# Own places in the timetable for the first and last samples, shares on ScalarE, and four statistics ahead of the branch

## The chip, the cores and the metric

The kernel runs on one core of a Trainium2 chip. The metric is the device time of one execution in microseconds. An execution contains one launch; the profiled execution gives both its own time and the span from its first to its last recorded instruction.

## The reference

The input `x` has 16 samples of 256 channels and 64x64 pixels, in float32. Two layers are computed, each added to its input. Both begin with a group normalisation (32 groups of 8 channels).

```python
def _L0_conv_ref(x, g_norm, w_qkv, w_out, b_out, g_out):   # linear attention
    xn = rmsnorm(x, g_norm)                                # over channels
    qkv = einsum('oc,bchw->bohw', w_qkv, xn)               # 3 x 4 heads x 32
    q = softmax(q, axis=-2); k = softmax(k, axis=-1)
    context = einsum('bhdn,bhen->bhde', k, v)
    out = einsum('bhde,bhdn->bhen', context, q * scale)
    return rmsnorm(einsum('oc,bchw->bohw', w_out, out) + b_out, g_out)

def _L1_conv_ref(x, router_w, router_b, dw_w, dw_b, pw_w, pw_b):
    prob = softmax((mean(x, axis=(2, 3)) @ router_w.T + router_b) / 2.0)
    # the best 2 of 4 experts per sample; each expert:
    #   depthwise 3x3 convolution + bias, gelu, 256x256 pointwise + bias
    # the output is their sum, weighted by the renormalised probabilities

x = x + _L0_conv_ref(_gn(x), ...)
x = x + _L1_conv_ref(_gn(x), ...)
```

## The kernel before, in words

A short head loads sample 0 into the ring, scales the query, key and value weights, and tests whether the attention logits are small enough. A branch then runs `pipelined_path`, which is the path taken here.

Everything in that path is one list of steps. A step belongs to a sample `b` and to one of five phases. Phases `in`, `q` and `out` go over eight tiles `g` of 512 pixels; phase `route` is once a sample; phase `x` goes over four quarters `j` of 1024 pixels.

- `in`: `load_a`, `stats` (one `bn_stats` per 128 channels, L264), then `mean` to `bias`, the scale and bias of the first group norm.
- `q`: `load_b`; `norm` (L305 on VectorE or L307 on ScalarE); transposes `turn_x` (L315); `x_sq` (L322) and `token` (VectorE, then a power on GpSimd, L242), which make the scale `r` of a pixel; `x_keep` (L331 or L333), `project` (L346), `evacuate` (the exponential, L354), `context` (L364), `q_sum` (L374), `q_norm` on GpSimd (L379), `q_turn` (L387) and `q_keep` (L390). After the last tile `mix_a` to `mix_c` make one matrix `mw` of the context and the output weights.
- `out`: `load_x1` into the ring, `attend` (L440), `out_sq` (L448), `out_scale` (L241 and GpSimd L242), `out_norm` (L461 on ScalarE or L463 on VectorE), `out_turn` (L468), `out_add` (L477), `sq_sums` (L484).
- `route`: second group norm, router, and the choice of taps.
- `x`: channels 0 to 127 get their depthwise convolution on TensorE: `pad0` (ScalarE), `lay` and `spread` (DMAs through DRAM), `conv` (L719), `gelu0` (L727). Channels 128 to 255 get it on VectorE: `pad1`, `start`, and eight `tap` steps for each of two experts (L741, 1024 pixels each), then `gelu1` (L750). `pick` mixes the pointwise weights of the four experts; `lay_pw` and `spread_pw` lay half of them out; `pw` is the pointwise matmul (parts 0 and 1 at L768, parts 2 and 3 with 32 rows at L779), `residual` adds bias and input, `store` writes.

There is one order for all engines: every step has a place, and the steps are issued in the order of their places. Each engine, and SP's queue of DMAs, then works through its own instructions in that order. A place is counted in units of which a tile has `SLOT` = 8 and a sample 64:

```python
    def place(row):
        phase, b, g, key = row[:4]
        pace = 1 if phase in ("route", "x") else slots[b][phase] / SLOT
        return starts[b][phase] + slots[b][phase] * g + PLAN[key] * pace
```

`PLAN` holds one number for each kind of step, the same for all samples, and offsets for whole phases of the first three samples and the last two. So while sample `b` is in its phase `x`, the `out` phase of `b+1` or `b+2` and the `q` phase of `b+2` or `b+3` are in progress. The first samples have nothing ahead of them to overlap with, and the last have nothing behind.

Three shares depend on the sample. `norm` and `x_keep` are on VectorE for samples below `EARLY` = 3, else on ScalarE. `out_norm` is on VectorE except in the last sample. In the last sample the input is added by TensorE in a fifth part of `pw` (part 4, a matmul with the identity, L774), and `residual` is an activation on ScalarE (L793) in place of the add on VectorE (L795).

Of the kernel before, what the change touches and what calls it, by code (L numbers as in the profile page):

```python
# [10 lines left out]
FP = mybir.dt.float32  # L11
# [5 lines left out]
P = 128  # L17
# [30 lines left out]
EARLY = 3  # L48
# [5 lines left out]
    "load_x1": 2.47, "mean": 1.04, "means": 4.69, "dev": 5.07, "devs": 8.24, "scale": 8.52,  # L54
    "bias": 12.08, "in_lead": 22.23, "norm0": -5.91, "norm1": -3.77, "turn_x0": 0.61, "x_sq0": 1.9,
    "x_sq1": 2.11, "turn_x1": 1.64, "x_sq2": 2.36, "x_sq3": 2.68, "token": 3.59, "x_keep0": 5.41,
    "x_keep1": 5.42, "x_keep2": 5.2, "x_keep3": 5.22, "project0": 3.62, "evacuate0": 5.48,
    "project1": 4.85, "evacuate1": 5.69, "project2": 5.61, "evacuate2": 6.6, "project3": 5.69,
    "evacuate3": 6.83, "context": 7.87, "q_sum": 8.01, "q_norm": 13.4, "q_turn": 15.77,
    "q_keep": 16.04, "mix_a": 8.41, "mix_turn": 9.67, "mix_v": 10.33, "mix_vv": 11.49, "mix_b": 12,  # L60
    "mix_out": 12.87, "mix_c": 13.33, "mix_lead": 15.68, "attend0": -0.16, "out_sq0": 0.33,
    "out_sq1": 0.7, "out_scale0": 1.35, "out_norm0": 2.44, "attend1": 0.39, "out_sq2": 1.3,
    "out_sq3": 1.47, "out_scale1": 2.38, "out_norm1": 3.76, "out_turn0": 4.83, "out_add0": 6.02,
    "sq_sums0": 6.68, "out_turn1": 5.56, "out_add1": 6.85, "sq_sums1": 7.24, "sums1": 7.53,
    "means1": 7.77, "scale1": 8.7, "router": 9.48, "route": 9.99, "choose": 12.08,
    "pick_taps": 16.41, "route_lead": 22.29, "pick_rows0": 12.27, "pick_rows1": 15.38,
    "pick_row_bias": 13.7, "weigh": 19.29, "pick_bias": 20.19, "pick000": 1.5, "pick100": 11.76,
    "pick001": 2.67, "pick101": 11.83, "pick002": 5.78, "pick102": 15.2, "pick003": 8.9,
    "pick103": 15.49, "pick010": 1.98, "pick110": 13.36, "pick011": 3.58, "pick111": 15.09,
    "pick012": 4.61, "pick112": 15.41, "pick013": 6.8, "pick113": 16.18, "lay_pw": 10.27,  # L70
    "spread_pw": 12.95, "taps0": 6.17, "taps1": 1.71, "taps2": 2.27, "taps3": -4.16, "taps4": 9.52,
    "taps5": -1.21, "taps6": -1.21, "taps7": 11.56, "pad1": -10.11, "start0": -3.22, "tap01": 0.77,
    "tap02": 1.13, "tap03": 1.92, "tap04": 2.35, "tap05": 2.68, "tap06": 3.77, "tap07": 5.22,
    "tap08": 6.68, "gelu10": 10.88, "start1": 3.82, "tap11": 5.21, "tap12": 6.65, "tap13": 8.35,
    "tap14": 9.77, "tap15": 11.78, "tap16": 12.05, "tap17": 13.11, "tap18": 13.97, "gelu11": 15.52,
    "pad00": 1.66, "pad01": 2.92, "lay": 4.37, "spread0": 6.43, "conv0": 10.64, "gelu00": 11.57,
    "spread1": 6.19, "conv1": 11.39, "gelu01": 12.09, "spread2": 5.8, "conv2": 10.58,
    "gelu02": 11.06, "spread3": 6.79, "conv3": 12.01, "gelu03": 12.46, "spread4": 6.78,
    "conv4": 13.04, "gelu04": 14.02, "spread5": 7.96, "conv5": 13.16, "gelu05": 14.2,
    "spread6": 9.37, "conv6": 13.42, "gelu06": 14.64, "spread7": 10.33, "conv7": 13.97,  # L80
    "gelu07": 14.66, "pw00": 16.91, "pw01": 17.04, "pw02": 18.17, "pw03": 18.59, "pw10": 19.2,
    "pw11": 20.88, "pw12": 21.41, "pw13": 21.48, "residual00": 20.87, "residual01": 25.47,
    "residual02": 27.17, "residual03": 27.67, "store0": 29.36, "residual10": 23.57,
    "residual11": 25.64, "residual12": 27.45, "residual13": 28.04, "store1": 33.91,
    "in_first": 2.74, "in_more": 1.74, "q_first": 9.11, "out_first": 7.86, "out_more": 15.48,
    "q_less": 0.26, "load_a0": -16.2, "load_a1": -8.65, "load_b0": -17.65, "load_b1": -7.1,
    "stats0": -4.87, "stats1": -3.45, "load_weights": 21.49, "scale_weights": -2.89,
    "spread_taps00": -8.7, "spread_taps01": -1.56, "spread_taps10": 1.5, "spread_taps11": 5.1,
    "end_pw00": 16.45, "end_pw01": 18.13, "end_pw02": 14.45, "end_pw03": 15.46,
    "end_residual00": 23.47, "end_residual01": 25.21, "end_residual02": 26.09,  # L90
    "end_residual03": 28.08, "end_pw10": 17.51, "end_pw11": 19.09, "end_pw12": 14.97,
    "end_pw13": 16.08, "end_residual10": 28.63, "end_residual11": 28.83, "end_residual12": 29.05,
    "end_residual13": 30.35, "x_0": -0.07, "x_1": -0.03, "x_2": -0.04, "x_e1": -0.24, "x_e2": -0.02,
    "route_0": 1.22, "route_1": -0.07, "route_2": 0, "route_e1": 0.66, "route_e2": 0.04,
    "out_0": -0.91, "out_1": 0.05, "out_2": -0.02, "out_e1": 0.4, "out_e2": 0.22, "q_0": -0.72,
    "q_1": 1.29, "q_2": 0.04, "q_e1": -0.03, "q_e2": 0, "in_0": 8.12, "in_1": 4.22, "in_2": 0.93,
# [1454 lines left out]
```

## Time and profile before

| | |
|---|---|
| time, median of 3 runs | 2724.26 us (2723.83 to 2724.53) |
| the profiled execution's own time | 2722.39 us |
| its span | 2720.7 us |
| mean granted TensorE clock | 0.992 |
| TensorE busy | 2636.2 us, 97% |
| VectorE busy | 2417.5 us, 89% |
| ScalarE busy | 2083.4 us, 77% |
| GpSimd busy | 767.4 us, 28% |
| DMA moved | 394.77 MB, mean 145 GB/s |

Below, PE is TensorE, DVE is VectorE, ACT is ScalarE, POOL is GpSimd and SP is the queue that issues the DMAs. A line of the groups gives the source line, engine, operation, output and input tiles with their shapes, the number of instructions, the busy time with the mean of one in ns, and the idle time just before them with what ended most of it. A line of the waits reads "who waited <- for whom: us in total, times, longest". A line of the timeline starts with start and duration. Matmuls are pipelined, so their durations overlap; the spacing of starts is the real cost. A float32 matmul leaves two records, a transpose one.

### The profile page before, as it was taken

How to read it: one execution, taken by the hardware profiler on the slowest of the kernel's cores; microseconds unless marked ns; L12 is line 12 of the kernel's file. 1: busy time of each engine (PE TensorE's matmuls, PEld its weight loads, DVE VectorE, ACT ScalarE, POOL GpSimd, SP SyncE). 2: the span in 40 equal slices, each digit the busy share in tenths (PEclk: the TensorE clock that was granted, in tenths of full speed). 3: DMA queues.
4: the chain of work that ended last, by engine and by line, in shares of the span. 5: the costliest groups of instructions: out<-in, count | busy, mean ns of one | idle time of the engine just before them, and what ended most of it. 6: DMA issues, size and time to landing. Idle time of an engine off the chain costs nothing.

```text
span 2720.7 us, 55294 instructions
## 1 busy us (share of the span) xinstructions
PE 2636.2 (97%) x19300; PEld 2257.1 (83%) x19300; DVE 2417.5 (89%) x4480; ACT 2083.4 (77%) x5230; POOL 767.4 (28%) x874
## 2 busy tenths in 40 slices
PE   6898999999999999999999999999999999998888
PEld 5787888888888888888888888888888888886677
DVE  6889998999989898898989989898898988889984
ACT  3576788887887888788787888888788788876543
POOL 2242232322323222232322323233222323232200
PEclk9999999999999999999999999999999999999989
DMA  4335454454545546355354545445454443525332
GB/s 155 113 125 148 141 170 153 133 167 155 154 146 158 158 144 184 129 162 170 125 170 153 155 155 158 155 143 173 143 159 154 145 135 123 150 85 140 118 110 89
DMA packets 229711, 394.77 MB, mean 145 GB/s; under 512 B 25904, under 2 KB 108336, under 8 KB 229424
## 3 DMA queue, kind: packets, MB, share of 16 engines
q1 hardware_dynamic: 228880, 390.75, 46.4%
q8 instruction: 156, 2.56, 0.4%
q14 instruction: 131, 1.07, 0.1%
q10 hardware_dynamic: 544, 0.39, 0.0%
HBM read 280.82 MB, written 110.23 MB: 144 GB/s over the span
## 4 chain that ended last, share of the span: by engine, by line
PE 88%; DVE 7%; ACT 1%; issue 1%; DMA 1%; POOL 1%; SPq 0%; ACTq 0%; POOLq 0%; DVEq 0%
PE pw L779 17%; PE pw L768 16%; PE dw L719 15%; PE pq L346 14%; PE pc L364 8%; PE po L440 8%; PE px L315 4%; PE tr L468 4%; DVE acc L741 3%; PE ptq L387 2%; DMA ring<-in_x 1%; DVE ring L477 1%; DVE ring L795 1%; PE pw L774 1%; DVE st L264 0%
## 5 line engine op out<-in xcount | busy, mean ns | idle before, releaser
L741 DVE SCALAR_TENSOR_TENSOR acc<-pd,ds,acc 128x1024 f32<-128x1024 f32 x1024 | 1304.7, 1284 | 14.7 <-ACT acc L734 10.9
L242 POOL TENSOR_TENSOR s<-s,mhalf 128x2 f32<-128x2 f32 x256 | 212.2, 831 | 1103.2 <-DVE s L241 1085.4
L346 PE MATMUL pq<-wqkv_n,xg 128*128 128x256 f32 x2048 | 504.7, 384 | 0.9
L719 PE MATMUL dw<-xr,taps 128*128 128x256 f32 x2048 | 489.2, 381 | 8.4 <-ACT xr L727 6.2
L768 PE MATMUL pw<-h,pw 128*128 128x256 f32 x2048 | 480.7, 383 | 15.6 <-ACT h L750 10.0
L779 PE MATMUL pw<-xr,psp 32*128 32x256 f32 x8192 | 485.1, 382 | 0.0
L779 PEld LDWEIGHTS pw<-xr,psp 32*128 32x128 f32 x8192 | 405.9, 185 | 66.7 <-issue 47.3
L768 PEld LDWEIGHTS pw<-h,pw 128*128 128x128 f32 x2048 | 382.2, 191 | 74.3 <-ACT h L750 12.4
L719 PEld LDWEIGHTS dw<-xr,taps 128*128 128x128 f32 x2048 | 374.5, 190 | 58.9 <-ACT xr L727 11.4
L346 PEld LDWEIGHTS pq<-wqkv_n,xg 128*128 128x128 f32 x2048 | 370.8, 192 | 58.2 <-ACT xt L333 11.7
L322 ACT ACTIVATE jx<-px 128x256 f32<-128x256 f32 x512 | 195.3, 381 | 193.6 <-PE px L315 173.9
L354 ACT ACTIVATE e<-pq,r 128x256 f32<-128x256 f32 x512 | 219.8, 470 | 134.5 <-PE pq L346 119.7
L242 POOL TENSOR_TENSOR r<-r,mhalf 128x4 f32<-128x4 f32 x128 | 186.1, 1454 | 448.8 <-DVE r L241 425.5
L795 DVE SCALAR_TENSOR_TENSOR ring<-pw,bs,ring 128x256 f32<-128x256 f32 x480 | 214.5, 475 | 66.1 <-PE pw L768 37.5
L440 PE MATMUL po<-mw,qt 128*128 128x256 f32 x1024 | 253.1, 381 | 0.7 <-DVE ring L795 0.7
L727 ACT ACTIVATE xr<-dw,bv 128x256 f32<-128x256 f32 x512 | 219.5, 478 | 40.1 <-PE dw L719 38.1
L364 PE MATMUL pc<-xt,e 128*128 128x257 f32 x1024 | 245.9, 382 | 3.6 <-DVE xt L331 3.4
L484 ACT ACTIVATE sqj<-ring,nm 128x512 f32<-128x512 f32 x256 | 185.9, 726 | 70.7 <-DVE ring L477 68.9
L477 DVE SCALAR_TENSOR_TENSOR ring<-tr,gout,ring 128x512 f32<-128x512 f32 x256 | 188.8, 746 | 41.5 <-PE tr L468 37.0
L448 ACT ACTIVATE junk<-po 128x256 f32<-128x256 f32 x512 | 196.5, 384 | 25.5 <-PE po L440 20.7
L364 PEld LDWEIGHTS pc<-xt,e 128*128 128x128 f32 x1024 | 189.4, 191 | 29.0 <-issue 3.4
L440 PEld LDWEIGHTS po<-mw,qt 128*128 128x128 f32 x1024 | 190.2, 190 | 28.0 <-issue 2.0
(144 smaller groups left out, 3569.6 us busy)
## 6 DMA issues: line engine op xcount, KB each, us to landing
xr<-lay SPq DMA_DIRECT2D x1024, 66.0 KB
ring<-in_x SPq DMA_DIRECT2D x256, 256.0 KB
out<-ring SPq DMA_DIRECT2D x128, 512.0 KB
xa<-in_x SPq DMA_DIRECT2D x240, 256.0 KB
xb<-in_x SPq DMA_DIRECT2D x240, 256.0 KB
lay<-pd SPq DMA_DIRECT2D x64, 594.0 KB
psp<-layp SPq DMA_DIRECT2D x128, 128.0 KB
layp<-pw SPq DMA_DIRECT2D x16, 256.0 KB
```

Of the source, the lines that this page charges most:

```text
L242: nc.gpsimd.tensor_tensor(out_t, out_t, mhalf[:, :n], ALU.pow)
L346: nc.tensor.matmul(pq, xg[:, k, c * P : (c + 1) * P], wqkv[:, k, : 2 * HID], start=(k == 0), stop=(k == KH - 1),)
L354: nc.scalar.activation(live["e", b, g][:, c], live["pq", b, g, c // 2][:, c % 2], AF.Exp, scale=live["r", b, g][:, c : c + 1],)
L364: nc.tensor.matmul(live["pc", b], live["e", b, g][:, c, HID:], xt[g % 2][:, c], start=(g == 0 and c == 0), stop=(g == NG - 1 and c == CG - 1),
L440: nc.tensor.matmul(po[:, c], qt[:, n * P : (n + 1) * P], live["mw", b], start=True, stop=True)
L477: nc.vector.scalar_tensor_tensor(xin, live.pop(("tr", b, g, k)), gout[:, k : k + 1], xin, ALU.mult, ALU.add, accum_out=live["sm", b][:, 0, ...
L719: nc.tensor.matmul(po, live[f"taps{g}", b][:, d * P : (d + 1) * P], rows3[:, :, d : d + W // 2], start=(d == 0), stop=(d == 1),)
L727: nc.scalar.activation(live["xr", b, j, g][:, 0 : GT // 2], po, AF.Gelu, bias=live["bv", b][:, g : g + 1])
L741: nc.vector.scalar_tensor_tensor(acc, pd1[j % 2][:, t // 3 : t // 3 + QR, t % 3 : t % 3 + W], live["ds", b][:, i, t : t + 1], acc, ALU.mul ...
L768: nc.tensor.matmul(po[q], live["pw1", b][:, part, ms], h[:, q % 2, q // 2], start=begin, stop=end,)
L779: nc.tensor.matmul(po[q], live["psp", b][band, g, ms], live["xr", b, j, g][band, 0 : GT // 2], start=begin and g % 4 == 0, stop=end and g ...
L795: nc.vector.scalar_tensor_tensor(xo, po, bs, xo, ALU.add, ALU.add)
```

## The change

Every step of samples 0, 1, 2, 14 and 15 may have a place of its own, under a key `step@sample.tile` (samples 14 and 15 are called `e2` and `e1`); 958 of them are given. The common places in `PLAN` are also given anew. The steps of the VectorE convolution become a phase `v`, which can start and pace differently from `x` in the last sample. `out_norm` of samples 0 and 1, and `norm` and `x_keep` of sample 2, move to ScalarE. In the last sample part 4 of `pw` and the activation in `residual` remain for quarters 0 and 1 only; quarters 2 and 3 add on VectorE. Four of the sixteen `bn_stats` of sample 0 are issued before the branch. The statistics tile `st` has one buffer instead of two.

```diff
-EARLY = 3
+EARLY = 2
+HEAD_STATS = 2
...
 PLAN = {
...
-    "token": 3.59, "spread_taps01": -1.56, "load_weights": 21.49, "load_x1": 2.47, "store0": 29.36,
+    "token": 3.74, "spread_taps01": 17.3, "load_weights": 1.12, "load_x1": 3.37, "store0": 33.89,
...
+    "pw04": 14.44, "pw14": 33.82, "x_last": 15.94, "v_last": 15.78, "v_e1": 1.28,
+    "tap18@e2.3": 12.77, "start0@e1.3": -5.22, "token@2.7": 4.71, "pw01@e2.3": 19.93,
...
+    "x_keep0@0.2": 5.43, "out_add0@2.2": 6.67, "x_keep1@1.1": 5.53,
 }
...
+    live["st", 0] = st_0
+
     def stats(b, g, k):
-        st = live["st", b] if ("st", b) in live else new(small, [P, KH, NG, 6], "st", b, bufs=2)
+        st = live["st", b] if ("st", b) in live else new(small, [P, KH, NG, 6], "st", b, bufs=1)
...
     def out_norm(b, g, hf):
...
-        if b == NB - 1:
+        if b in (0, 1, NB - 1):
             for c in range(2):
                 nc.scalar.activation(ob[:, c], po[:, c], AF.Copy, scale=s[:, c : c + 1])
...
     def pointwise(b, j, m, part):
...
-        n = 5 if b == NB - 1 else 4
+        n = 5 if by_pe(b, j) else 4
...
+    def by_pe(b, j):
+
+        return b == NB - 1 and j < NQ // 2
...
     def residual(b, j, m, q):
...
-        if b == NB - 1:
+        if by_pe(b, j):
             nc.scalar.activation(xo, po, AF.Identity, bias=bs)
         else:
             nc.vector.scalar_tensor_tensor(xo, po, bs, xo, ALU.add, ALU.add)
...
-                at("in", b, g, f"stats{k}", stats, b, g, k)
+                if b or g >= HEAD_STATS:
+                    at("in", b, g, f"stats{k}", stats, b, g, k)
...
-                    at("x", b, j, f"tap{i}{t}", tap1, b, j, i, t)
+                    at("v", b, j, f"tap{i}{t}", tap1, b, j, i, t)
...
-                for part in range(5 if b == NB - 1 else 4):
+                for part in range(5 if by_pe(b, j) else 4):
...
+        if b == NB - 1:
+            slot |= {"x": PLAN["x_last"], "v": PLAN["v_last"]}
-        start = {"x": PERIOD * b}
+        start = {"x": PERIOD * b, "v": PERIOD * b}
...
     def place(row):
         phase, b, g, key = row[:4]
-        pace = 1 if phase in ("route", "x") else slots[b][phase] / SLOT
-        return starts[b][phase] + slots[b][phase] * g + PLAN[key] * pace
+        pace = 1 if phase in ("route", "x", "v") else slots[b][phase] / SLOT
+        own = PLAN.get(f"{key}@{nears[b]}.{g}", PLAN[key])
+        return starts[b][phase] + slots[b][phase] * g + own * pace
...
+    st_0 = head.tile([P, KH, NG, 6], FP, name="st_0")
...
         nc.vector.tensor_tensor(sq, wqkv[:, :, : 2 * HID], wqkv[:, :, : 2 * HID], ALU.mult)
+        for g in range(HEAD_STATS):
+            for k in range(KH):
+                nc.vector.bn_stats(st_0[:, k, g], ring[g // 2][:, k, g % 2])
         pn = pp.tile([P, 2 * HID], FP, name="pn_n")
```

## Prediction

> **What bounds the kernel now.** I read the page first, for the engines' shares over the span and in its 40 slices:
>
> ```profile
> span 2720.7 us, 55294 instructions
> ...
> PE 2636.2 (97%) x19300; PEld 2257.1 (83%) x19300; DVE 2417.5 (89%) x4480; ACT 2083.4 (77%) x5230; POOL 767.4 (28%) x874
> ...
> PE   6898999999999999999999999999999999998888
> DVE  6889998999989898898989989898898988889984
> PEclk9999999999999999999999999999999999999989
> ```
>
> TensorE is full in all but the first few and last few slices. Next, the table of windows, cut where the slices change:
>
> ```profile
> 60.00:100.00 40.00, 30.95 (x156) 24.86 (x155) 34.04 (x101) 16.44 (x53) 9.60 (x11) 0.91 0.34 112
> 100.00:180.00 80.00, 79.58 (x455) 70.87 (x454) 68.87 (x182) 61.38 (x211) 30.47 (x35) 1.00 0.39 129
> 180.00:225.00 45.00, 32.20 (x155) 26.78 (x154) 44.03 (x109) 26.32 (x80) 17.15 (x23) 0.85 0.35 111
> 1300.00:1462.00 162.00, 161.93 (x1202) 139.58 (x1201) 147.38 (x270) 133.51 (x333) 47.39 (x53) 1.00 0.50 155
> 2425.00:2500.00 75.00, 66.03 (x523) 52.80 (x521) 72.90 (x139) 48.50 (x118) 23.59 (x24) 1.00 0.43 120
> 2500.00:2540.00 40.00, 38.42 (x341) 31.06 (x342) 34.30 (x47) 26.67 (x65) 8.37 (x10) 1.00 0.41 133
> 2540.00:2616.00 76.00, 59.16 (x446) 47.71 (x446) 72.19 (x127) 36.04 (x70) 15.89 (x19) 0.92 0.36 106
> 2616.00:2713.00 97.00, 96.14 (x800) 80.77 (x800) 60.90 (x50) 42.22 (x81) 2.42 (x5) 0.98 0.28 98
> ```
>
> Columns: length, busy us (instructions) of PE, its loads, DVE, ACT and POOL, granted clock, DMA share, GB/s. The middle is TensorE alone: `mw` is written at 1128.3, 1290.5 and 1452.7, a period of 162.2 us, so one unit of the timetable (64 a sample) is 2.53 us, and only fewer TensorE cycles can shorten it. VectorE is full in 180 to 225 and again in 2425 to 2616, with TensorE waiting. After 2616 TensorE is full again. The waits and TensorE's timeline say for what:
>
> ```profile
> PE tr L468 <- DVE ob L463: 11.3, 4, 5.4
> ...
> PE pw L768 <- ACT h L750: 10.0, 4, 7.8
> ```
> ```profile
> 212.16 0.69 PE L468 MATMUL tr<-ident,ob 128*128 128x128 f32 x2 [5.35 <-DVE ob L463]
> 216.36 0.69 PE L468 MATMUL tr<-ident,ob 128*128 128x128 f32 x2 [3.51 <-DVE ob L463]
> ```
>
> In the head `out_turn` waits for `out_norm` (L463), late in VectorE's queue; in the tail `pw` waits for the gelu behind the last tap.
>
> Busy time overstates pipelined matmuls, so I counted steady spacings (a 128x256 part of 8 records is 1.73 us) along the order of the timetable. From 26.10 (first transpose) to 100.37 (end of the first `attend`) the order holds 57.2 us and took 74.3: 17.1 lost. From 178.2 to 224.5 it holds 28 and took 46.3: 18.3 lost. From `mix_out` of sample 15 (2425.3) to its first `pw` (2616.4) it holds 157 to 159 and took 191: about 33 lost. Nothing else is large.
>
> **The change, part by part.** I sorted both timetables by their places and kept a running total per engine, with durations from the groups (start-to-start where the engine is dense).
>
> ```profile
> L463 DVE TENSOR_TENSOR ob<-po,s 128x512 f32<-128x512 f32 x240 | 163.6, 682 | 4.5 <-POOL s L242 4.4
> L331 DVE TENSOR_SCALAR xt<-px,r 128x256 f32<-128x256 f32 x96 | 40.2, 476 | 4.8 <-POOL r L242 4.2
> L461 ACT ACTIVATE ob<-po,s 128x256 f32<-128x256 f32 x32 | 13.5, 479 | 6.5 <-POOL s L242 6.4
> L333 ACT ACTIVATE xt<-px,r 128x256 f32<-128x256 f32 x416 | 168.6, 485 | 25.6 <-POOL r L242 22.6
> L307 ACT ACTIVATE xg<-xb,bi,sc 128x512 f32<-128x512 f32 x208 | 169.4, 814 | 0.0
> ```
>
> *Head statistics.* Four `bn_stats` go before the branch, where VectorE waits 2.2 us for the `pn` matmuls (7.65 to 9.88). Four at 0.60 are 2.4, so the branch comes 0.2 later and the queue behind it is 2.4 shorter. Input tiles land every 0.68 us, the fourth by about 7.5 and the last by 15.7, an estimate from the spacing of the load issues; both are early enough. Gain 2.2. If the tiles were late it would be 0.
>
> *First sample's attention, 26 to 100.* Before, a step costs 7.3 us against 6.5 of TensorE work: transpose 0.45, four squares 2.0, `r` on VectorE 0.2 and POOL 1.2, then `q_norm` 1.03 behind it, `q_turn` and `context` 2.4, and only then the next transposes. In the new order the next `turn_x` stands ahead of `context`, so the loop is about 5.8 and TensorE's 6.5 rules: five steps by 0.8 is 4. VectorE's excess over TensorE up to the last `context` falls from 5.6 to 0.2, because one of the four `spread_taps` (2.5) and two statistics of sample 2 (0.6 each) move behind it. `mix_a` to `mix_c` gets about 2 us longer, with `q_sum` and statistics between its steps. Sum: 17.1 lost becomes about 9, gain 8 (4 to 11). On SP the 25 weight loads pass ahead of sample 1's `xa` loads; they end near 25, `xa` lands near 31, and its first reader is due near 37 (41.4 before). Without that cover it would cost about 3.
>
> *Shares moved to ScalarE.* Between `mix_a` of sample 1 and `out_turn` of step 3 of sample 1, VectorE had 65.3 us against TensorE's 47.2: excess 18.1, the loss seen. Of the 65.3, 16.3 move (9 `out_norm` at 0.60, 9 `norm` at 0.50, 16 `x_keep` at 0.40), leaving 49, about level. But ScalarE now has, from `evacuate` of step 6 to that `out_turn`, 70.1 us (12 `out_norm` at 0.75, 10 `norm` at 0.70 and 16 `x_keep` at 0.36 are 21.8 of it) against TensorE's 58.5. So the queue that is late next is ScalarE's, by 11.6; with a little for semaphores I take 13, gain 5. Bounds: 11 if TensorE runs ahead of it, and -8 if every one of the 131 instructions waits for its semaphore, which cost 0.1 each at the first tile (squares 0.51 apart instead of 0.40). I take the dense value, since this queue would be full. The Trainium skill ("ScalarE: Activation LUTs", rules for kernel authors) speaks against the move: plain multiplies and adds belong on VectorE. Per operation the rows agree (0.75 against 0.60). From its price for an ACTIVATE, about (N+335)/1.2 ns less 93 of overlap, the moved 21.8 would be an estimated 23.1, the loss 14 instead of 13. But staying on VectorE costs 18, so in this stretch the rule loses. After it the moved work is covered by the TensorE-bound middle.
>
> *Middle.* No work is removed, but the order changes. Between two `pw` parts of 32 rows (L779) stand `q_turn` and `context` once a sample. Two halves take 1.94 each against 3.66 together, and the matmul after each block is about 0.05 slower: 0.27 a split. Sorted, there are 9 blocks a sample before and 8 after; over 11 samples 3 us. Bounds: 0, and 5 with the 10, 12 and 11 blocks near sample 13 falling to 8, 8 and 9. Running totals of VectorE and ScalarE stay below TensorE's. `st` with one buffer costs nothing: its writer and reader are in one queue and the reader comes first.
>
> *Tail.* Part 4 of `pw` goes for the last two quarters: four times the 2.01 us that the chain shows for 8 records of L774, all after 2616, where TensorE is the bound: 8.0. Its adds move to VectorE, 16 at 0.40; there VectorE is busy 60.9 of 97, so they hide until the last 8, which replace 8 on ScalarE (3.3 us) one for one. The VectorE-bound stretch stays: from `mix_c` to the last `pick` 180 us before and after, and the excess over TensorE is 23.8 before and 23.2 after. Of the other 11 us that VectorE idled there I take 1 as saved (between -3 and 5). `x_last` and `v_last` only reorder. Gain 9.
>
> Sum: 2.2 + 8 + 5 + 3 + 9 = 27. The profiled execution took 2722.4 (span 2720.7), so about 2695; the median lies 1.9 above that execution, so 2697.
>
> **Rivals.** (1) *ScalarE's queue is the new bound in full*: the -8 above instead of 5. It also waits in order for POOL's `s` (6.4 us over 6 waits in L461's row). 2697 + 13 = 2710. For: 70 against 58. Against: the same operations ran dense in the middle.
> (2) *The stalls close completely*: the attention loss falls to 4, the ScalarE loss to 5, and the tail saves 4 more: 2697 - 17 = 2680. For: nothing else in the totals exceeds TensorE. Against: two queues equally full seldom interlock without waits.
> (3) *Slower, through SP*: in the new order `load_x1` of every even step stands behind `lay`, which SP issues only when ScalarE has padded (SP waits 647.9 us in all for that). If the input tile then lands after its `out_add`, VectorE stalls four times a sample. From `pad01` to `out_add` are 5.8 units, 14.8 us; `lay` and the loads take 1.3 to issue and a tile 5.5 to 6.6 to land, so it decides from about 7 us of lateness, and then 1 us is worth 4 a sample, some 50 in all: 2745. Against: that margin, and no wait for this tile shows before.
> (4) *Nothing changes*: most own places could sort to the same order. They do not where it counts (`context` behind `turn_x`, 34 operations on another queue). 2724.
>
> **How the numbers follow.** A measurement of this kernel tells about 0.2% (5.4 us) from no change. Forecast, 2688 to 2706: 0.60. Rival 1, 2706 to 2717: 0.16. Rival 2, 2674 to 2688: 0.15. No change: 0.04. Slower: 0.05. Faster is 0.91. The range leaves out a tenth on either side: 2679 to 2714.
>
> **What would show it.** Right: TensorE's first transpose near 23.9; steps of 6.5 to 6.6 after it; a first `pw` about 15 us earlier; in 180 to 215 VectorE no longer full and waits of `tr` for ACT `ob` L461 in place of DVE `ob`; a period near 161.9; 32 records of L774 instead of 64; a last stretch shorter by 8. Wrong: ScalarE waits longer than 15 us in the head; VectorE waiting for `ring` loads; a longer period in the middle; or a stretch before the last sample's first `pw` that is not 190 but 170.

## The result, and the profile after

The changed kernel took 2710.0 us (median of 5, 2709.0 to 2711.2) against 2724.3 us for the kernel before (2722.3 to 2725.1): a ratio of 0.9948, with a 95% interval of 0.9934 to 0.9963. The forecast of "faster" came true. The time lies in the range (2679 to 2714), but above the interval that was called the likeliest (2688 to 2706): the gain is 14 us where 27 were forecast. The profiled execution took 2710.0 us and its span is 2708.3, against 2720.7 before: 12.4 us to be explained.

The head of the page after, with the same rows that were shown of before:

```profile
span 2708.3 us, 55405 instructions
...
PE 2629.2 (97%) x19268; PEld 2258.3 (83%) x19268; DVE 2422.8 (89%) x4416; ACT 2126.3 (79%) x5326; POOL 831.5 (31%) x874
...
PE   6898999999999999999999999999999999998988
...
DVE  7778898999989899898999989899898998989996
...
PEclk9999999999999999999999999999999999999999
```

Busy time hardly moved: VectorE has 5 us more, although 80 operations left it for ScalarE and only 16 adds came, and GpSimd has 64 us more with the same 874 instructions. What moved is seen by stage (columns: length, busy us and instructions of TensorE, its loads, VectorE, ScalarE and GpSimd, granted clock, DMA share, GB/s):

```profile
60.00:100.00 40.00, 32.64 (x151) 26.55 (x150) 32.47 (x96) 16.35 (x54) 9.84 (x10) 0.87 0.32 107
100.00:180.00 80.00, 79.42 (x453) 70.00 (x452) 53.25 (x154) 74.56 (x246) 30.88 (x36) 1.00 0.36 119
180.00:225.00 45.00, 36.17 (x170) 27.76 (x169) 41.43 (x90) 43.37 (x119) 19.43 (x23) 0.96 0.42 136
...
1300.00:1462.00 162.00, 161.33 (x1202) 139.83 (x1201) 149.52 (x272) 133.88 (x334) 51.31 (x53) 1.00 0.49 155
...
2611.00:2701.00 90.00, 88.90 (x768) 74.38 (x768) 69.41 (x67) 40.46 (x74) 2.46 (x5) 0.97 0.33 110
```

In 60 to 100 TensorE is still not full, and its clock is lower than before (0.87 against 0.91). In 100 to 180 TensorE is full as before, and ScalarE nearly so (74.56 of 80, before 61.38). In 180 to 225 ScalarE is the full queue (43.37 of 45), where it was VectorE. The middle is not shorter: 161.33 busy in 162 means that TensorE now waits there. The last stretch is shorter.

To place the 12.4 us, take steps that have the same TensorE work ahead of them in both orders, and subtract their starts. The lead of the changed kernel over the one before, in us:

| step | before | after | lead |
|---|---|---|---|
| first transpose | 26.10 | 23.91 | 2.2 |
| q_turn of step 6, sample 0 | 87.02 | 77.12 | 9.9 |
| q_turn of step 7, sample 0 (behind the mix chain) | 102.96 | 98.78 | 4.2 |
| turn_x of step 0, sample 2 | 169.61 | 166.31 | 3.3 |
| first pw | 239.25 | 236.28 | 3.0 |
| mix_c of sample 15 | 2425.73 | 2427.26 | -1.5 |
| first pw of sample 15 | 2616.39 | 2611.36 | 5.0 |
| end of the last TensorE instruction | 2713.04 | 2700.39 | 12.7 |
| end of the span | 2720.7 | 2708.3 | 12.4 |

So the lead grows to 9.9 us, loses more than half within 22 us, is spent altogether in the middle, and is earned anew behind `mix_c` of sample 15, in the last 281 us. The expectations below also speak of the loss at a step: its start less the TensorE work that the order puts ahead of it.

The waits of TensorE that are new (line waited for, us in total, times, longest), from the stage of 165 to 320 us and then from 300 to 2300:

```profile
PE tr L709 <- ACT ob L702: 5.3, 3, 3.7
PE dw L960 <- DMA xr<-lay: 1.9, 2, 1.5
```
```profile
PE tr L709 <- DVE ring L1040: 8.2, 13, 0.8
```

The first is the forecast change of hands: `out_turn` now waits for ScalarE's `out_norm` (L702) and no longer for VectorE's. The second is what stands behind ScalarE's padding. The third was not in the forecast at all: once in each of 13 samples a transpose waits for VectorE's residual add (L1040). Before, the middle had no TensorE wait.

### The profile page after: what moved, and what is told of

Its sections match the earlier page's. It is cut to its first block, busy times and chain, and to the rows that moved or that the text cites. A ratio compares the mean times of both kernels' runs of the same rounds, so it can differ in the third digit from the quotient of the medians.

```text
span 2708.3 us, 55405 instructions
## 1 busy us (share of the span) xinstructions
PE 2629.2 (97%) x19268; PEld 2258.3 (83%) x19268; DVE 2422.8 (89%) x4416; ACT 2126.3 (79%) x5326; POOL 831.5 (31%) x874
## 4 chain that ended last, share of the span: by engine, by line
PE 81%; DVE 12%; ACT 3%; issue 2%; DMA 1%; POOL 1%; SPq 0%; DVEq 0%; ACTq 0%; POOLq 0%
PE pq L587 15%; PE pw L1020 14%; PE dw L960 14%; PE pw L1009 13%; PE po L681 7%; PE pc L605 7%; DVE acc L982 6%; PE tr L709 4%; PE px L556 4%; PE ptq L628 2%; DVE ring L1040 1%; DMA xr<-lay 1%; DVE ring L718 1%; DVE st L505 1%; DVE ob L704 0%
## 5 line engine op out<-in xcount | busy, mean ns | idle before, releaser
L982 DVE SCALAR_TENSOR_TENSOR acc<-pd,ds,acc 128x1024 f32<-128x1024 f32 x1024 | 1323.6, 1301 | 9.2 <-ACT acc L975 4.8
L481 POOL TENSOR_TENSOR s<-s,mhalf 128x2 f32<-128x2 f32 x256 | 241.2, 943 | 1201.8 <-DVE s L480 1143.7
L960 PE MATMUL dw<-xr,taps 128*128 128x256 f32 x2048 | 480.4, 381 | 9.9 <-DMA xr<-lay 3.8
L587 PE MATMUL pq<-wqkv_n,xg 128*128 128x256 f32 x2048 | 479.3, 383 | 0.2
L587 PEld LDWEIGHTS pq<-wqkv_n,xg 128*128 128x128 f32 x2048 | 378.9, 192 | 50.6 <-DVE ring L718 3.2
L481 POOL TENSOR_TENSOR r<-r,mhalf 128x4 f32<-128x4 f32 x128 | 195.4, 1527 | 377.2 <-DVE r L480 265.1
L1040 DVE SCALAR_TENSOR_TENSOR ring<-pw,bs,ring 128x256 f32<-128x256 f32 x496 | 221.8, 475 | 64.9 <-PE pw L1009 51.2
```

The lines of the kernel that those rows point to most:

```text
L481: nc.gpsimd.tensor_tensor(out_t, out_t, mhalf[:, :n], ALU.pow)
L587: nc.tensor.matmul(pq, xg[:, k, c * P : (c + 1) * P], wqkv[:, k, : 2 * HID], start=(k == 0), stop=(k == KH - 1),)
L960: nc.tensor.matmul(po, live[f"taps{g}", b][:, d * P : (d + 1) * P], rows3[:, :, d : d + W // 2], start=(d == 0), stop=(d == 1),)
L982: nc.vector.scalar_tensor_tensor(acc, pd1[j % 2][:, t // 3 : t // 3 + QR, t % 3 : t % 3 + W], live["ds", b][:, i, t : t + 1], acc, ALU.mul ...
L1040: nc.vector.scalar_tensor_tensor(xo, po, bs, xo, ALU.add, ALU.add)
```

## The experiments

Each ratio is to the kernel before, measured with it (medians of 2722.6 to 2723.7); the changed kernel's is 0.9948. In some runs a line was added to the timetable, so that their line numbers are one higher.

**1. The spread_taps behind the mix chain.** The changed kernel's mix chain of sample 0, on TensorE, and what VectorE does just ahead of it (start, length, operation, wait in brackets):

```profile
85.61 0.41 PE L646 MATMUL pt<-ident,cn 128*128 128x128 f32 x2 [3.45 <-DVE cn L640]
85.86 1.55 PE L556 MATMUL px<-ident,xg 128*128 128x128 f32 x8
87.27 1.22 PE L657 MATMUL pv<-cx,wqkv_n 128*128 128x128 f32 x4
88.92 1.19 PE L670 MATMUL pm<-wout,ct 128*128 128x256 f32 x2 [0.43 <-ACT jx L563]
90.63 3.78 PE L681 MATMUL po<-mw,qt 128*128 128x256 f32 x8 [0.52 <-DVE mw L673]
94.21 4.74 PE L587 MATMUL pq<-wqkv_n,xg 128*128 128x256 f32 x16
```
```profile
82.33 2.55 DVE L460 SCALAR_TENSOR_TENSOR tab<-dwc,piece,tab 128x32 f32<-128x32 f32 x9
...
84.98 0.48 DVE L640 TENSOR_SCALAR cn<-pc,rec 128x256 f32<-128x256 f32 x1
```

`mix_a` (L640) stands behind a `spread_taps` of 2.55 us, and TensorE waits 3.45 us for it. Then 8 records of `po` take 3.78 us, where a later 8 take 1.89, and 16 of `pq` take 4.74 instead of 3.62.

```
-    "spread_taps00@0.7": -2.7,  "spread_taps01@0.7": 2.37,  "spread_taps10@0.7": 3.96,  "spread_taps11@0.7": 9.3,
+    "spread_taps00@0.7": 13.4,  "spread_taps01@0.7": 16,    "spread_taps10@0.7": 18.5,  "spread_taps11@0.7": 21,
```

> The changed kernel, with the four spread_taps of the first sample (VectorE, about 2.5 us each, 10 us in all) placed behind mix_c of that sample instead of ahead of mix_a. Theory A: in the changed kernel the attention loop gained about 8 us, and 5.4 of it were lost again between the last context and the first attends, because VectorE stands full of spread_taps there while TensorE waits and then runs at a granted clock of 0.5. Then mix_turn of sample 0 comes at about 78 instead of 85.6, the first attend at full clock (8 records in 1.9 us instead of 3.8), q_turn of step 7 at 88 to 90 instead of 98.8, and the first pw at 228 to 231 instead of 236.3; the kernel takes 2702 to 2705 us. Theory B: the queue of ScalarE, full from 160 to 236, sets the first pw whatever happens before it; then q_turn comes early as above, but the first pw stays at 234 to 236 and the time at 2708 to 2711.

Measured: 2706.2 us (2705.6 to 2706.8), ratio 0.9940 (0.9926 to 0.9954). `mix_turn` at 79.7, q_turn of step 7 at 90.95 (7.8 earlier than in the changed kernel), first `pw` at 229.9 (6.4 earlier), end of the span 4.5 earlier. So theory A holds in its mechanism, though q_turn, the clock and the time (2702 to 2705) stayed short of it, and theory B falls: ScalarE's full queue does not set the first `pw` by itself, and of 7.8 us gained before 100 us 4.5 arrive at the end. The first attend still took 3.56 us, so the clock was not cured, and 2.9 us went back at 100 to 105, where `context` waits for `x_keep` behind a `spread_taps`.

**2. The block of `choose`, `pick_taps` and `pick_rows0` broken up.** In the middle the three stand side by side on VectorE (4.5 us) ahead of `residual10`, which frees the bank that the transpose wants.

```
-    "pick_taps": 14.53,  "pick_rows0": 14.59,
+    "pick_taps": 16.4,   "pick_rows0": 15.6,
```

> The changed kernel, with pick_taps and pick_rows0 of the middle samples (3 to 13) placed a few steps later, so that of the 4.5 us that choose, pick_taps and pick_rows0 take in one block on VectorE only choose stands ahead of residual10. Theory A: this block is why TensorE's transposes tr wait 0.6 us once a sample for VectorE's adds into ring, and it is what ate the gain of the fewer 32-row blocks in the middle. Then the wait goes, the period falls from 162.4 to 161.7 or 161.8, mw of the last sample comes at about 2420 instead of 2427.3, and the kernel takes 2702 to 2705 us. Theory B: the middle is longer because VectorE's and GpSimd's instructions are slower side by side (taps 1301 ns instead of 1284); then the period stays at 162.3 to 162.4. Theory C: the period falls, but the last stretch up to the first pw of the last sample is VectorE's and takes the gain back; then 2708 to 2711.

Measured: 2721.1 us (2715.9 to 2724.0), ratio 0.9991 (0.9983 to 1.0000). None of the three. The wait of `tr` is gone from the middle samples, and another took its place, longer (waits of TensorE from 820 to 2300 us):

```profile
PE px L556 <- DVE s L480: 11.2, 8, 1.5
PE pq L587 <- DVE ring L718: 2.0, 9, 0.2
```

The period rose from 162.4 to 163.5. The moved 1.5 us of work made VectorE's queue later behind it (in one sample the next `out_norm` starts at 1003.42 instead of 1002.55), and `px`, about 22 us on, waits for a bank that an `out_norm` frees. The slack that I had seen at the block did not exist behind it.

**3. The end alone.** The kernel before, with part 4 of `pw` gone from the last two quarters.

```
-        n = 5 if b == NB - 1 else 4
+        n = 5 if by_pe(b, j) else 4
...
-        if b == NB - 1:
+        if by_pe(b, j):
```

> The kernel before, with one part of the change alone: for the last two quarters of the last sample part 4 of pw (the identity matmuls) is left out, and their residual adds are done on VectorE; the timetable stays that of before. Theory A: four times 2.01 us of TensorE go where TensorE is the bound, and the adds hide: 8.0 us less, 2716 us, the stretch after the first pw of the last sample 88 to 89 instead of 96.7. Theory B: the adds on VectorE stand behind the taps and hold the last stores back: 3 to 5 us less, 2719 to 2721.

Measured: 2716.7 us (2716.0 to 2719.2) against 2723.1, ratio 0.9978 (0.9969 to 0.9986): 6.4 us, between the two theories and nearer to A. From the first `pw` of sample 15 to the end of the span it is 98.0 us, against 104.3 before and 96.9 in the changed kernel. The last 8 adds hide as forecast. About half of what is missing can be seen: without the identity matmuls TensorE comes to two of the last `conv` before their tiles have landed.

```profile
2687.85 4.04 PE L719 MATMUL dw<-xr,taps 128*128 128x256 f32 x16 [0.49 <-DMA xr<-lay]
2692.17 1.10 PE L719 MATMUL dw<-xr,taps 128*128 128x256 f32 x4 [0.28 <-DMA xr<-lay]
```

In the changed kernel, whose last quarter has its own places, these waits do not appear. Up to the end of the last TensorE instruction the stretch is 6.1 us shorter here and 7.6 us shorter there.

**4. The shares alone.** The kernel before, its timetable unchanged.

```
-EARLY = 3
+EARLY = 2
...
-        if b == NB - 1:
+        if b in (0, 1, NB - 1):
```

> The kernel before, with another part alone: norm and x_keep of sample 2 and out_norm of samples 0 and 1 go to ScalarE; the timetable stays that of before. Theory A: moving the shares takes VectorE's excess of 18 us away and leaves ScalarE an excess of about 12 in the stage from 180 to 236: first pw at 233 to 236 instead of 239.3, 3 to 5 us less, 2719 to 2721. Theory B: ScalarE's queue also carries the padding that the first conv needs, so what VectorE's queue gains is lost again behind pad0 and lay: first pw at 238 to 242, 2723 to 2727.

Measured: 2725.3 us (2722.3 to 2727.7), ratio 1.0006 (1.0000 to 1.0013); first `pw` at 241.6 instead of 239.3. Theory B. One wait changed its name and kept most of its size: 11.3 us of `tr` for VectorE's `ob` before, and in this kernel, from 165 to 320 us:

```profile
PE tr L468 <- ACT ob L461: 8.5, 6, 2.6
```

**5. The shares taken back.** The changed kernel with all its places, the shares on VectorE as before.

```
-EARLY = 2
+EARLY = 3
...
-        if b in (0, 1, NB - 1):
+        if b == NB - 1:
```

> The changed kernel, with the shares back where they were: norm and x_keep of sample 2 and out_norm of samples 0 and 1 on VectorE again; all places as in the changed kernel. Alone in the old timetable the move to ScalarE gave nothing (2725 against 2723). Theory A: the new places need it: with the shares on VectorE its excess of 18 us over TensorE in the stage from 180 to 225 comes back and ScalarE's goes; first pw at 240 to 246 instead of 236.3, 2714 to 2719 us. Theory B: the two queues are equally full and it does not matter which carries the shares: first pw within 2 us of 236, 2708 to 2712.

Measured: 2737.8 us (2735.9 to 2738.3), ratio 1.0050 (1.0036 to 1.0064): 28 us slower than the changed kernel and 14 slower than before, far beyond theory A. The period from `mw` of sample 1 to that of sample 2 is 162.6 us instead of 143.1. Its stage and its waits (180 to 225, then 165 to 345 us):

```profile
180.00:225.00 45.00, 31.28 (x151) 26.02 (x150) 36.54 (x99) 26.62 (x79) 13.77 (x18) 0.83 0.31 100
```
```profile
PE tr L709 <- DVE ob L704: 10.5, 4, 3.3
PE pt L646 <- DVE cn L640: 3.7, 2, 2.7
PE po L681 <- DVE ring L718: 2.9, 1, 2.9
```

Here neither queue is full (36.54 and 26.62 of 45), and TensorE waits all the same, at a clock of 0.83, which points to engines that wait for each other in turn. With 4 and 5 together: the shares are worth nothing in the old places and 28 us in the new ones, and the rest of the change, its gains in the head and at the end included, costs 14 without the shares. The shares and the places cannot be priced one by one.

**6. The twelve route steps of the middle, `sums1` to `pick_bias`, at their old places** (the samples with own places keep theirs).

```
...
-    "router": 10.39, "route": 11.51, "choose": 14.5, "pick_taps": 14.53,
+    "router": 9.48,  "route": 9.99,  "choose": 12.08, "pick_taps": 16.41,
...
-    "pick_rows0": 14.59, "pick_rows1": 16.79, "pick_row_bias": 16.8, "weigh": 20.59, "pick_bias": 22.49,
+    "pick_rows0": 12.27, "pick_rows1": 15.38, "pick_row_bias": 13.7, "weigh": 19.29, "pick_bias": 20.19,
```

> The changed kernel, with the twelve steps from sums1 to pick_bias of samples 3 to 13 at the common places that they had before (choose 2.4 units, 6 us, earlier, and its block of 4.5 us on VectorE broken up). Theory A: the added 0.6 us of tr a sample is there because the block comes late, after VectorE has stood idle some 3 us for pw; placed early it fits into that idle time, the wait does not reappear elsewhere, the period is 161.7 to 161.9, and the kernel takes 2703 to 2706 us. Theory B: in the new common order VectorE is full for the 35 us from choose to the last pick whatever its order; then a wait of px or po for VectorE takes the place of that of tr, as when only pick_taps and pick_rows0 were moved, and the time is 2709 to 2722.

Measured: 2719.1 us (2716.4 to 2722.6), ratio 0.9984 (0.9978 to 0.9991), period 163.3 to 163.4. Theory B, though the wait is at another step than I named (820 to 2300 us; L710 is `tr`, L740 the matmul `means1`):

```profile
PE pg L740 <- ACT xt L575: 5.6, 6, 0.9
PE tr L710 <- DVE ring L1041: 3.6, 10, 0.4
```

Twice a place that looked too late was improved by itself, and twice the period grew by 1 us. Of the three orders the one with 0.6 us of wait was the best.

**7. Of the own places of samples 1 and 2, 57 dropped:** taps, padding, spread, `conv`, gelu, `pw` and `residual` of their second to fourth quarters. The three periods from 314 to 805 us are 163.7, 163.3 and 163.8 us, longer than the 162.4 of the rest.

```
-    "residual10@2.3": 24.68,
-    "pw02@2.2": 19.2,
-    "tap03@1.3": 1.86,
-    "residual13@2.2": 30.3,
...
```

> The changed kernel, without the own places of the steps of the second to fourth quarter of samples 1 and 2 (57 entries: taps, padding, spread, conv, gelu, pw and residual), which fall back to the common places. Theory A: the three periods from 314 to 805 us last 163.3 to 163.8 instead of 162.4 because of these places (10 blocks of 32-row matmuls instead of 8, and more waits): they fall to about 162.4, the kernel takes 2706 to 2707 us. Theory B: something else makes them long (VectorE still behind after the start); then 2709 to 2711. Theory C: the places were chosen for a reason there, and without them a wait appears in the stage from 230 to 500: 2711 to 2716.

Measured: 2711.7 us (2707.3 to 2712.3), ratio 0.9953 (0.9940 to 0.9967): no difference. The three periods are 165.8, 163.2 and 163.1, 1.3 us more in sum. Theory A falls; of B and C this run decides nothing. What the changed kernel's trace shows of these periods is a part of the answer: the 32-row `pw` stand in 11, 9 and 9 blocks instead of the 8 of the later samples, TensorE is busy 162.75, 162.31 and 162.38 us instead of 161.7, and it idles 1.0, 1.0 and 1.4 us instead of 0.7. Which of the places do this stays open.

**8. The mix chain fed.** The spread_taps as in 1 but further apart, and the first four `project` of sample 1 inside the chain.

```
-    "spread_taps00@0.7": -2.7, "spread_taps01@0.7": 2.37, "spread_taps10@0.7": 3.96, "spread_taps11@0.7": 9.3,
+    "spread_taps00@0.7": 20,   "spread_taps01@0.7": 26,   "spread_taps10@0.7": 32,   "spread_taps11@0.7": 38,
+    "project0@1.0": 2.2, "project1@1.0": 2.21, "project2@1.0": 2.7, "project3@1.0": 2.75,
```

> The changed kernel, with the four spread_taps of the first sample spread over the 50 us after mix_c (instead of close behind it as in the earlier run, which saved 5), and with the four project steps of the first tile of sample 1 (3.5 us of TensorE) placed inside the mix chain, ahead of mix_out and of the first attend. Theory A: TensorE then has work in the mix chain's waits, the granted clock stays at 1.0, the first attend runs in 1.9 us, and the 2.9 us that spread_taps cost behind the first attends stay saved: 9 to 11 us less at project of step 3 of sample 1 than in the changed kernel, 2699 to 2702 us. Theory B: the clock falls anyway, because the gaps remain: 2704 to 2706.

Measured: 2703.8 us (2703.6 to 2704.5), ratio 0.9929 (0.9915 to 0.9942). The chain:

```profile
82.00 1.89 PE L588 MATMUL pq<-wqkv_n,xg 128*128 128x256 f32 x8
...
85.89 1.89 PE L682 MATMUL po<-mw,qt 128*128 128x256 f32 x8
```

`po` takes 1.89 us instead of 3.78, no matmul waits for `ct` or `mw`, and q_turn of step 7 starts at 87.61, 11.2 us earlier than in the changed kernel. Theory A's mechanism is shown; its time (2699 to 2702) is not reached, because 5.2 of the 11.2 are given back by 130 us and 6.5 are left at the end.

**9. ScalarE's order behind it.** As 8, with `evacuate0` to `evacuate3` of that tile ahead of the first attend's squares.

```
+    "evacuate0@1.0": 3.45, "evacuate1@1.0": 3.5, "evacuate2@1.0": 3.6, "evacuate3@1.0": 3.65,
```

> As the run that spread the spread_taps and fed the mix chain with four project steps (2703.8), and in addition the four evacuate steps of the first tile of sample 1 stand ahead of the squares of the first attend on ScalarE, which stood idle for 4.35 us there while two context blocks later waited for them. Theory A: the 5 us that were given back between 88 and 130 us (loss 27.3 growing to 32.4) are that order on ScalarE: loss at context of step 4 of sample 1 at 28 to 30, first pw at 226 to 229, 2699 to 2702 us. Theory B: they are VectorE's, which is 90% busy in 100 to 130 with the spread_taps: 2703 to 2705 us as before.

Measured: 2703.2 us (2702.5 to 2704.4), ratio 0.9925 (0.9911 to 0.9939). Not to be told from run 8. The two waits for `e` went, and the loss at context of step 4 is still 30.7: theory B.

**10. Own places of the last samples' pw and residual dropped.** From `mix_c` of sample 15 to its first `pw` the waits of VectorE were, before and after:

```profile
DVE ring L795 <- PE pw L779: 3.4, 3, 1.4
DVE ring L795 <- PE pw L768: 2.8, 3, 1.3
```
```profile
DVE ring L1040 <- PE pw L1020: 1.2, 1, 1.2
...
DVE ring L1040 <- PE pw L1009: 0.7, 1, 0.7
```

VectorE, the bound of this stretch, waited 6.2 us in residual adds that came up before their `pw` was done; after the change 1.9.

```
-    "pw01@e2.3": 19.93,
-    "pw02@e1.2": 18.01,
-    "residual00@e2.3": 20.18,
-    "residual13@e2.2": 29.76,
...
```

> The changed kernel, without the own places of 54 pw and residual steps of samples 14 and 15, which fall back to the common places. In the stretch from mix_c of sample 15 to its first pw, VectorE is the bound in both kernels: it waited 8.9 us there before, 6.2 of it in adds that stood ahead of their pw in its queue, and 4.5 after, and the stretch went from 190.7 to 184.1 us. Theory A: the own places of pw and residual took those waits away: without them VectorE waits 4 to 7 us more for pw, the stretch is 188 to 191 us and the kernel takes 2714 to 2717 us. Theory B: the stretch is shorter because of the taps of samples 14 and 15 or the pace of the last sample: 2709 to 2711 us.

Measured: 2715.6 us (2709.9 to 2715.7), ratio 0.9964 (0.9951 to 0.9978). Its profile is of an execution of 2710.4 us, in which the first 100 us were 3.7 us faster than in the changed kernel's profile (q_turn of step 7 at 95.10; the last section tells why), so the tail is compared by its own stretches. The stretch takes 187.7 us instead of 184.1, and from `mix_c` to the end it is 286.4 instead of 281.0. VectorE's waits in 2425 to 2612:

```profile
DVE ring L718 <- PE tr L709: 4.7, 4, 2.8
DVE ring L1040 <- PE pw L1020: 2.3, 2, 1.8
```

So the own places of these steps are worth 5.4 us, about theory A's size. Its mechanism is not what came back: the waits are for `tr` more than for `pw`.

**11. The head statistics taken back.**

```
-HEAD_STATS = 2
+HEAD_STATS = 0
```

> The changed kernel with the four head statistics back behind the branch. Theory A: 2.2 us at the first transpose (26.1 instead of 23.9), carried to the end, as every other gain in the first 100 us was: 2711.5 to 2713 us. Theory B: a wait further on takes them back: 2709.5 to 2710.5.

Measured: 2712.5 us (2707.5 to 2714.3), ratio 0.9955 (0.9942 to 0.9969). First transpose at 26.43, 2.5 us later, and the end of the span 2.5 later. Theory A in both numbers, though by the times alone, 2.5 us apart, the two kernels are hardly told from each other.

**12. The spread_taps once more apart.** As 9, each between the two `out_scale` of one of steps 3 to 6.

```
-    "spread_taps00@0.7": 20,   "spread_taps01@0.7": 26,   "spread_taps10@0.7": 32, "spread_taps11@0.7": 38,
+    "spread_taps00@0.7": 37.2, "spread_taps01@0.7": 44.8, "spread_taps10@0.7": 52, "spread_taps11@0.7": 59,
```

> As the run before it with fed mix chain and early evacuate steps (2703.2), with the four spread_taps moved on once more: in that run they stood at 92 to 120 us, the first ahead of the token scale that GpSimd, x_keep and q_norm wait for; now each stands between the two out_scale steps of one later tile (steps 3 to 6 of sample 0), where VectorE waits 1.6 us for ScalarE's squares. Theory A: the 4.4 us that were given back between 87 and 130 us were theirs, and the new places cost about nothing: loss at context of step 4 of sample 1 at 27 instead of 30.7, 2699 to 2701 us. Theory B: any 10 us more on VectorE between 100 and 180 us are paid in waits of out_turn or q_turn, or the stage from 180 takes them back: 2702 to 2704 us.

Measured: 2702.8 us (2702.1 to 2704.4), ratio 0.9927 (0.9913 to 0.9940). The loss at context of step 4 is 28.8 instead of 30.7, the first `pw` comes at 226.5 instead of 228.1, and the end of the span 1.0 earlier than in 9. By the time theory B: the places were part of the 4.4 us, and waits of `out_turn` for ScalarE (0.53 to 0.96 each) stand in for the rest. Runs 8, 9 and 12 are the fastest kernels here, 6 to 7 us below the changed one, and cannot be told from each other.

## Why the prediction was right, and where its sum was not

By the table of leads, the terms of the sum and what they came to:

| term | forecast | measured |
|---|---|---|
| head statistics | 2.2 | 2.2 |
| first sample's attention | 8 (4 to 11) | 2.0: 7.7 won in the loop, 5.7 lost in the mix chain |
| shares moved to ScalarE | 5 (-8 to 11) | -1.2 |
| middle | 3 (0 to 5) | -4.5 |
| tail | 9 | 14.2: 6.6 ahead of the first `pw`, 7.6 behind it |
| after the last matmul | 0 | -0.3 |

That the time lies in the range is luck in part: without the 5 us by which the tail beat its forecast it would have been 2715.

*Head statistics.* The number is right, and run 11 shows that it reaches the end. Its parts are not: the branch's test came 0.85 us later (`fits` at 11.19 instead of 10.34) and not 0.2, and 0.7 us of small constants, which had stood among the statistics at 19.04 to 19.70, moved behind them.

*Attention of sample 0.* The step that I costed was right: the first steps take 6.51 us, exactly TensorE's, in place of 7.3. The step that failed is the sentence on `mix_a` to `mix_c`, "about 2 us longer". I had counted that a `spread_taps` moves behind the last `context`, and had not seen that it lands ahead of `mix_a`, which everything behind it waits for. Nor had I priced what the waits leave behind. TensorE then ran at half its clock for 10.2 us, though busy for most of them:

```profile
86.24:96.48 10.24, 9.29 (x27) 6.87 (x25) 7.39 (x18) 3.80 (x16) 3.67 (x4) 0.50 0.39 130
```

The five rows from `px` to `pq` at run 1 took 4.6 us more than the same records at full clock (3.78 - 1.89, 4.74 - 3.62, 1.55 - 1.04, 1.22 - 0.71 and 1.19 - 0.59). The kernel before lost here too, only less: between the two q_turn TensorE waited 3.7 us in it and 6.5 after the change, and the half clock cost about 1.9 us (8 records of `pc` in 3.77 us instead of 1.9) and 4.6. The two differences, 2.8 and 2.7, are the 5.7 us of lead that went. Runs 1 and 8 show the cause: the chain with shorter waits, then fed, starts q_turn of step 7 by 7.8 and 11.2 us earlier. The Trainium skill ("TensorE: Matmul & The Clock Gate", Part 1) has the clock fall to half after an idle window of about 3.4 us and return after one busy window. The wait of 3.45 us would fit, but in run 1 the clock fell too, at 83.9 us, and its waits from 60 us up to there are only 0.78, 0.44, 0.71 and the first 0.3 of one of 0.52 us; the measurement decides. By the skill's rule one window at half the clock would cost an estimated 1.7 us; here it was three windows' length.

*Shares.* The arithmetic of the queue was right (ScalarE full from 180 to 225, the wait renamed to ACT `ob`), and so was the gain up to there: the lead rose from 3.3 to 8.8 at 214 us (attend of step 3, 222.81 to 214.06). The step that failed is "After it the moved work is covered by the TensorE-bound middle". By the first `pw` the lead was back at 3.0. ScalarE's padding ends only 0.5 us earlier than before (`lay` is issued at 205.38 instead of 205.87), so TensorE, 8.8 us ahead, now waits for what stands behind it: 1.9 us for `xr`, 1.2 for the taps and for `qt`, and about 1.7 at half the clock (0.50 from 229.6 to 233.0). So the term came to 0 instead of 5, and another 0.9 us went in small ScalarE waits from 135 to 165, where `out_norm` of sample 0 now stands. This is rival 1's queue, with its wait one step further on than its text has it, and with -1.2 where rival 1 had -8. What I had not thought of is run 5: the price of a share depends on the places around it.

*Middle.* The mechanism that I named is there: 8 blocks of 32-row matmuls a sample instead of 9, and the TensorE busy time of a period fell from 162.12 to 161.73, 0.39 where I had 0.27. (That the block alone made the 0.39 no run isolated.) Two windows, before and after:

```profile
803.90:966.10 162.20, 162.12 (x1205) 139.78 (x1203) 147.58 (x272) 133.72 (x334) 47.38 (x53) 1.00 0.51 155
```
```profile
1129.80:1292.20 162.40, 161.73 (x1204) 140.14 (x1203) 149.89 (x271) 134.25 (x335) 51.70 (x54) 1.00 0.49 154
```

The step that failed is "running totals of VectorE and ScalarE stay below TensorE's". A running total over a sample does not see a block of 4.5 us ahead of one add on which a bank depends. The wait of 0.6 us a sample ate the gain (period 162.4 against 162.2). Another 4.5 us went in the three periods from 314 to 805. Run 7 cleared one suspect; more 32-row blocks and more waits are seen there, and which places cause them is not known. The lead was at its lowest, -3.4, at 2290 us; the last period before `mix_c` of sample 15 gave some back (160.8 us, before 162.1).

*Tail.* The 8.0 for part 4 were 7.6 (run 3, without the new places, has 6.1), and 32 records of L1015 remain, as forecast. The undersized term is the 1 us (-3 to 5) that I gave to the 11 us in which VectorE idled. 4.4 of it were saved (8.9 us of waits became 4.5), and VectorE has 2.1 us less to do in the stretch (179.5 became 177.3): together the 6.6. Run 10 gives the places of `pw` and `residual` 5.4 us, of which 3.6 lie in this stretch and 1.8 behind it. I had kept this term small because the totals did not show what the idle time was made of; the waits of VectorE in that window, shown at run 10, would have.

*Rivals.* Rival 1's time, 2710, is the measured one, but most of the shortfall against 2697 is in the mix chain and the middle. Rival 2 falls: the losses did not close. Rival 3 falls: from 60 us on VectorE waited for a `ring` load once, for 2.5 us. Rival 4 falls with the 14 us. Of the signs of being right, the first transpose (23.91), the steps of 6.5, the waits for ACT `ob` and the 32 records came true; the first `pw` came 3.0 us earlier and not 15, and the period was not 161.9 but 162.4. The longer period in the middle, which I had listed as a sign of being wrong, came true.

## What to carry to other kernels

Two timetables are compared by the lead at steps with equal work ahead of them: it shows in one table which gains survive, and here it showed one of 9.9 us of which 5.7 were gone 22 us later. A gap on TensorE cost itself here and the slower matmuls behind it, so look at what stands on the other engines just ahead of the operation that ends it, and fill the gap with independent matmuls. Where every queue is nearly full, a move of work and the order around it are one change: here the shares alone gave about 0 us, all the rest without them minus 14, and both together 14.

## What the runs showed of the hardware

When the clock falls and returns differs from one execution to the next. In run 2, whose TensorE instructions up to here are those of the changed kernel, and with the same wait of 3.45 us, it stayed at half for 3.4 us and not for 10.2:

```profile
85.11:88.53 3.42, 3.22 (x14) 2.96 (x14) 2.96 (x6) 1.66 (x7) 1.05 (x1) 0.50 0.27 77
88.53:91.94 3.41, 2.60 (x11) 2.02 (x12) 2.90 (x8) 0.91 (x5) 1.23 (x1) 1.00 0.44 111
```

and q_turn of step 7 came at 95.3 instead of 98.8. In all fourteen traces of this case every stretch at half clock lasts 3.41 us or two or three times that, on a grid of 3.41 us that begins at another moment in each execution. The Trainium skill says of the window in the same part that it is free-running, so that the moment of the change varies from run to run; the rows agree. How idle such a stretch has to be can be read from the same traces, with TensorE's busy time added up on each grid from about 30 to 2680 us. The clock fell 72 times, always behind a stretch of 3.41 us with 1.4 us or more of idle time, and it fell behind every one with more than 1.91 us. It returned 72 times, never behind a stretch with more than 0.61 us. Several short waits can thus do what one long wait does, as in run 1 (1.46 us idle from 80.5 to 83.9). Some kernels with the gap scatter more (three times of run 10 are at 2715.6 and two at 2710) than the one without it (2703.6 to 2704.5 in run 8), which would fit, though the other executions have no trace. So 4 us between two profiles with such a gap are not yet an effect of the edit.

VectorE and GpSimd are slower side by side. Before and after, groups by operation (busy us, mean ns of one):

```profile
L741 DVE SCALAR_TENSOR_TENSOR acc<-pd,ds,acc 128x1024 f32<-128x1024 f32 x1024 | 1304.7, 1284 | 14.7 <-ACT acc L734 10.9
L242 POOL TENSOR_TENSOR s<-s,mhalf 128x2 f32<-128x2 f32 x256 | 212.2, 831 | 1103.2 <-DVE s L241 1085.4 <-PE dw L719 7.3 <-DVE dt L559 5.0
```
```profile
L982 DVE SCALAR_TENSOR_TENSOR acc<-pd,ds,acc 128x1024 f32<-128x1024 f32 x1024 | 1323.6, 1301 | 9.2 <-ACT acc L975 4.8
L481 POOL TENSOR_TENSOR s<-s,mhalf 128x2 f32<-128x2 f32 x256 | 241.2, 943 | 1201.8 <-DVE s L480 1143.7 <-PE dw L960 30.1 <-DVE g L743 9.6
```

The same 1024 taps took 18.9 us more and the same 256 scales 29 us more. In the traces the taps and GpSimd's instructions overlap for 287 us before and 419 after, and the taps with no GpSimd instruction beside them last the same in both, 1273 and 1272 ns on average (710 and 597 of them). So the new order puts the two side by side more often, which agrees with the skill's "GPSIMD Engine Reference" (Specifications), that the two engines share SBUF interfaces where VectorE reads two inputs. It explains why VectorE has more busy time with less to do. No run here isolated it.
